# A recurrence stage rewritten: sums on column groups, W x kept in order of time, the state's product added on VectorE

## The chip, the cores and the metric

The kernel runs on one core of a Trainium2 chip. The metric is the device time of one execution in microseconds; the figure for a kernel is the median of its runs. The engines named below are TensorE (PE in the profile, its weight loads PEld), VectorE (DVE), ScalarE (ACT), GpSimd (POOL) and SyncE (SP), whose queue issues most DMAs. Tiles live in SBUF with 128 partitions, results of products in PSUM[...].

## The reference, cut to what matters

The input is 4 images of 128 channels and 64 x 64 places, all in float32. Layer 0, a convolution with a selective scan, and the attention of layer 1 come first and are not touched. The change is in the last line:

```python
t = t + _L1_attn_ref(_ln_t(t), ...)        # t: 4 images, 4096 tokens, 128 channels
t = t + _L1_ffn_ref(_ln_t(t), W, V, gamma, beta)

def _ln_t(v, eps=1e-5):                    # norm over the 128 channels of a token
    m = mean(v, -1); s = var(v, -1)
    return (v - m) / sqrt(s + eps)

def _L1_ffn_ref(x, W, V, gamma, beta):
    flat = (x @ W.T).reshape(4 * 4096, 128)
    mean, var = flat.mean(0), flat.var(0)  # per channel, over all tokens of all images
    Wx = (flat - mean) * rsqrt(var + 1e-5) * gamma + beta
    y = 0
    for t in range(4096):                  # lax.scan
        y = sigmoid(Wx[:, t] + y @ V.T)
        ys[t] = y
    return ys
```

So there are a norm over channels, a product with W (128 x 128), statistics of that product over all 16,384 tokens, and only then a recurrence in time whose every step needs the one before.

## The kernel before, in words

Channels lie on the 128 partitions and tokens along the free axis. Layer 0 and the attention (`_rational`) each run in an order written out by hand (`manual_schedule`: every engine issues in the order of the source). The attention walks through 4 images of 8 blocks of 512 queries; of a block it keeps A, 32 tiles of 128 keys x 512 queries. At a block's end ScalarE takes A in parts, `PARTS`, with a tanh and an exp for each part (L1384, L1385), and PE sums the weighted values (L1360, one product of 512 columns for each of the 32 tiles). After the last block its closing follows (L1252 to L1268: a copy, two products, a reciprocal, a GpSimd add and the store of the block to `x2` in HBM on SP's queue).

The last stage is `_chunked`. It is not under an order by hand: a planner puts the instructions of each engine in order by its costs. Its parts, in order of time:

- **Load.** X (128 x 4 x 4096) comes from `x2` by four DMAs of 2 MB on SP's queue (L170). The weights come on ScalarE's queue (L115).
- **Norms**, for 16 pieces of 1024 columns: the mean over channels is a product with a 128 x 128 matrix of 1/128 (`avg`; two products of 512 columns, L55), which leaves the mean on all partitions. DVE subtracts it out of PSUM (L1450), ACT squares (L1451), PE averages the squares in the same way (L55), ACT takes the logarithm and the exponential that make 1/sqrt (L70, L71), and DVE multiplies into xn (L1455), a copy of the normalised values *in order of time*: column index (step t, chunk c, image b).
- **Sums over W x:** 32 products of 512 columns with W (L1463), each read once out of PSUM by DVE's BN statistics (L1464) and dropped.
- **Scale:** the statistics are put together (L1466) to a scale and a shift per channel; the scale is multiplied into W, which PE transposes (L1474 to L1478, wsT).
- **Steps.** Time is cut into 64 chunks of 64 steps that run side by side: one step works on 64 chunks x 4 images = 256 columns, in two halves of 128 that form two independent streams. A chunk starts from 16 warm-up steps on the end of the chunk ahead of it. In each step PE adds W's product on xn and V's product on the state in one PSUM tile (L1501, L1513), and ACT takes the sigmoid with the shift as bias (L1514), written over xn. W's products do not need the state; they are issued 5 half-steps ahead.
- **Tail.** y is added to X in 16 pieces of 1024 columns, by turns on DVE and POOL (L1524), and each piece is stored by one DMA of 512 KB (L1527). Beside it a flag is worked out that says whether the warm-up had met the chunks' true ends and the attention's bounds held; `_general` runs where it does not.

Rows of other stages that are used for prices below: L671 (products of layer 0 with a 32-column weight, into column groups of one PSUM tile), L678 (ACT's copy out of PSUM to a strided place), L1230 (DVE's multiply of 512 columns with one operand in PSUM), L1243 (DVE's multiply-add of 512 columns), L1336 and L1349 (POOL's adds).

The functions:

Of the kernel before, what the change touches and what calls it, by code (L numbers as in the profile page):

```python
# [38 lines left out]
WARM = 16  # L39
QB = 512  # L40
PARTS = ((0, 4), (4, 12), (12, 20), (20, 32))
CLOSE_AT = (14, 16, 17, 18, 19, 20, 22)
NORM_AT = (15, 17, 19, 20)
QUERIES_AT = (24, 26)
# [100 lines left out]
@with_exitstack  # L145
def _bounded(
    ctx: ExitStack,
    tc: tile.TileContext,
    flag,
    x1,  # L150
    x, in_wT, conv_w, conv_b, sa_w, sa_b, xpT, xpR, dtwT, dtb, A_quads, Ds,
    on_g, on_b, n1_g, n1_b, out_wT, WtT, WxT, Wt, Wx, bh, Wa, ba, W, WT, VT, gamma, beta,
    out,
):
    nc = tc.nc
    const = ctx.enter_context(tc.tile_pool(name="fconst", bufs=1))
    dram = ctx.enter_context(tc.tile_pool(name="gdram", bufs=1, space=DRAM))
    k = _Consts(tc, const)
    x2 = dram.tile([B, P, L], F32, name="x2")

    with tc.manual_schedule():
        _layer0(tc, k, x, x1, in_wT, conv_w, conv_b, sa_w, sa_b, xpT, xpR, dtwT, dtb, A_quads, Ds,
                on_g, on_b, n1_g, n1_b, out_wT)
    top = const.tile([P, TOPS], F32, name="top")
    with tc.manual_schedule():
        _rational(tc, k, x1, x2, top, Wt, Wx, bh, Wa, ba)
    with tc.tile_pool(name="gresid", bufs=1) as resid:
        X = resid.tile([P, B, L], F32, name="X")
        for b in range(B):
            nc.sync.dma_start(X[:, b, :], x2[b])  # L170
        _chunked(tc, None, flag, top, X, k.ident, k.avg, k.ones, k.eps5, k.load, k.filled,
                 W, WT, VT, gamma, beta, out)


@with_exitstack
# [873 lines left out]
def _rational(ctx, tc, k, x1, x2, top, Wt, Wx, bh, Wa, ba):  # L1049
# [253 lines left out]
    for b in range(B):  # L1303
        upcoming = None
        for s in range(nq):
# [74 lines left out]
                else:  # L1380
                    held["first"] = held["first"], lower("B1", F, 1, E)

            for i, (lo, hi) in enumerate(PARTS):
                nc.scalar.activation(A[:, lo:hi, :], A[:, lo:hi, :], AF.Tanh, bias=b_a)  # L1384
                nc.scalar.activation(A[:, lo:hi, :], A[:, lo:hi, :], AF.Exp)  # L1385
                if i == 0:
                    if turned:

                        F = big.tile([P, 2, L], F32, name="F")
                        for c in range(nq):  # L1390
                            all_keys(F, upcoming, c)
                    ahead(0)
                if hi <= NOW or not more:
                    for jt in range(lo, hi):
                        weighted(jt)
                ahead(i + 1) if i + 1 < len(PARTS) else None
            if more:
                nc.vector.tensor_tensor(A[:, 0, :], held["A"][:, 0, :], held["A"][:, 1, :], ALU.add)
                first = held["first"]
# [17 lines left out]


@with_exitstack
def _chunked(ctx, tc, last, flag, top, X, ident, avg, ones, eps5, load, filled, W, WT, VT, gamma, beta, out):  # L1420

    nc = tc.nc
    wp = ctx.enter_context(tc.tile_pool(name="cw", bufs=1))
    big = ctx.enter_context(tc.tile_pool(name="cbig", bufs=1))
    w2 = ctx.enter_context(tc.tile_pool(name="cw2", bufs=2))

    w = load(wp, W, [P, P], "w")
    wT = load(wp, WT, [P, P], "wT")
    vT = load(wp, VT, [P, P], "vT")
    ga = load(wp, gamma, [P, 1], "ga")  # L1430
    be = load(wp, beta, [P, 1], "be")


    xn = big.tile([P, CT, NC * B], F32, name="xn")
    st = big.tile([P, B * L // MM, 6], F32, name="st")
    flat = xn.rearrange("p t c -> p (t c)")
    with tc.tile_pool(name="cps", bufs=2, space=PSUM) as ps2, tc.tile_pool(
        name="cpsm", bufs=1, space=PSUM
    ) as psm:
        with _ln_exp_table(tc, last):  # L1440
            for b in range(B):
                xb4 = xn.rearrange("p t (c b) -> p b c t", b=B)[:, b]
                for c in range(L // CH):
                    cols = slice(c * CH, (c + 1) * CH)
                    mean_ps = psm.tile([P, CH], F32, name="mean_ps")
                    var_ps = psm.tile([P, CH], F32, name="var_ps")
                    t1 = w2.tile([P, CH], F32, name="t1")
                    sq = w2.tile([P, CH], F32, name="sq")
                    _mm(nc, mean_ps, avg, X[:, b, cols], CH)
                    nc.vector.tensor_tensor(t1, X[:, b, cols], mean_ps, ALU.subtract)  # L1450
                    nc.scalar.activation(sq, t1, AF.Square)  # L1451
                    _mm(nc, var_ps, avg, sq, CH)
                    _rsqrt(nc, sq, var_ps, eps5)
                    nch = CH // CT
                    nc.vector.tensor_tensor(  # L1455
                        xb4[:, c * nch : (c + 1) * nch, :],
                        t1.rearrange("p (c t) -> p c t", t=CT),
                        sq.rearrange("p (c t) -> p c t", t=CT),
                        ALU.mult,
                    )  # L1460
            for m in range(B * L // MM):
                ps = ps2.tile([P, MM], F32, name="wx", tag="wx")
                nc.tensor.matmul(ps, wT, flat[:, m * MM : (m + 1) * MM], start=True, stop=True)  # L1463
                nc.vector.bn_stats(st[:, m, :], ps)  # L1464
        mv = wp.tile([P, 2], F32, name="mv")
        nc.vector.bn_aggr(mv, st.rearrange("p a s -> p (a s)"))  # L1466
        scale = wp.tile([P, 1], F32, name="scale")
        _rsqrt(nc, scale, mv[:, 1:2], eps5)
        nc.vector.tensor_tensor(scale, scale, ga, ALU.mult)
        shift = wp.tile([P, 1], F32, name="shift")  # L1470
        nc.vector.tensor_tensor(shift, mv[:, 0:1], scale, ALU.mult)
        nc.vector.tensor_tensor(shift, be, shift, ALU.subtract)

        nc.vector.tensor_scalar(w, w, scale, None, ALU.mult)  # L1474
        ws_ps = ps2.tile([P, MM], F32, name="ws_ps", tag="wx")
        nc.tensor.transpose(ws_ps[:, 0:P], w, ident)
        wsT = wp.tile([P, P], F32, name="wsT")
        nc.vector.tensor_copy(wsT, ws_ps[:, 0:P])  # L1478


    pst = ctx.enter_context(tc.tile_pool(name="cpst", bufs=7, space=PSUM))
    psf = ctx.enter_context(tc.tile_pool(name="cpsf", bufs=1, space=PSUM))
    half = NC * B // 2
    start = wp.tile([P, NC * B], F32, name="start")
    nc.vector.memset(start, 0.0)


    steps = []
    for i in range(WARM):
        t = CT - WARM + i  # L1490
        for lo, hi in ((B, half), (half, NC * B)):
            y = start[:, lo:hi] if i == WARM - 1 else w2.tile([P, half], F32, name="y", tag=f"y{lo}")[:, 0 : hi - lo]
            steps.append((xn[:, t, lo - B : hi - B], y, hi - lo, i == 0))
    for t in range(CT):
        for lo, hi in ((0, half), (half, NC * B)):
            steps.append((xn[:, t, lo:hi], xn[:, t, lo:hi], half, False))

    def project(i):
        rhs, _, n, alone = steps[i]
        ps = pst.tile([P, half], F32, name="wxs")  # L1500
        nc.tensor.matmul(ps[:, 0:n], wsT, rhs, start=True, stop=alone)  # L1501
        return ps

    AHEAD = 5
    queue = [project(i) for i in range(AHEAD)]
    prev = [None, None]
    for i, (_, y, n, alone) in enumerate(steps):
        if i + AHEAD < len(steps):
            queue.append(project(i + AHEAD))
        ps = queue.pop(0)  # L1510
        if not alone:
            state = start[:, (i % 2) * half : (i % 2 + 1) * half] if i in (2 * WARM, 2 * WARM + 1) else prev[i % 2]
            nc.tensor.matmul(ps[:, 0:n], vT, state, start=False, stop=True)  # L1513
        nc.scalar.activation(y, ps[:, 0:n], AF.Sigmoid, bias=shift)  # L1514
        prev[i % 2] = y


    for b in range(B):
        for c in range(L // CH):
            cols = slice(c * CH, (c + 1) * CH)  # L1520
            nch = CH // CT
            eng = nc.vector if c % 2 else nc.gpsimd
            xo = X[:, b, cols].rearrange("p (c t) -> p c t", t=CT)
            eng.tensor_tensor(  # L1524
                xo, xo, xn.rearrange("p t (c b) -> p b c t", b=B)[:, b, c * nch : (c + 1) * nch, :], ALU.add
            )
            nc.sync.dma_start(out[b, :, cols], X[:, b, cols])  # L1527
    gap = wp.tile([P, NC * B - B], F32, name="gap")
    nc.vector.tensor_tensor(gap, xn[:, CT - 1, 0 : NC * B - B], start[:, B:], ALU.subtract)
    worst = wp.tile([P, 1], F32, name="worst")  # L1530
    nc.vector.tensor_reduce(worst, gap, AX.X, ALU.max, apply_absolute_value=True)
    nc.vector.tensor_scalar(worst, worst, MEET, None, ALU.is_le)
# [3 lines left out]
    nc.vector.tensor_scalar(far, far, REACH, None, ALU.is_le)  # L1536
    nc.vector.tensor_tensor(worst, worst, far, ALU.mult)
    n_ps = psf.tile([1, 1], F32, name="n_ps")
    nc.tensor.matmul(n_ps, worst, ones[:, 0:1], start=True, stop=True)
    nc.vector.tensor_copy(flag, n_ps)  # L1540


# [66 lines left out]
```

## Time and profile before

| | us |
|---|---|
| median of 3 runs (lowest, highest) | 11821.63 (11802.34, 11826.4) |
| profiled execution, its own time | 11810.23 |
| its span | 11808.5 |
| of it, up to the end of the last softmax's sum | 11493.6 |
| closing and first of X | 15.4 |
| norms | 120.1 |
| sums over W x | 34.2 |
| scale | 5.3 |
| warm-up steps | 21.8 |
| 64 steps | 74.1 |
| tail | 44.0 |

The span is the time between the first and the last event that the profiler recorded; times within it are counted from its start. The page of the profile gives the busy time of every engine and cuts the span into 40 slices with a digit for each engine. The groups of instructions by line give a count, the busy time and the mean duration of one. A table of windows gives busy time, count, the granted TensorE clock (PEclk, 1.00 is full) and the DMA traffic of chosen stretches. A timeline lists the instructions in order of time: start, duration, engine, line, operation, written tile <- read tiles, shape, and in brackets the idle time before it and what ended that. "PE 10343.2 (88%)" on the page is the busy share of the whole span. The stage that is changed is the last 315 us of it.

### The profile page before, as it was taken

What the parts mean: (1) busy time and instruction counts of PE and PEld (TensorE: products, weight loads), DVE (VectorE), ACT (ScalarE), POOL (GpSimd) and SP (SyncE); (2) the same over time, 40 slices, a digit from 0 to 9 for tenths busy, and PEclk for the clock granted to TensorE, in tenths of its full rate; (3) what the DMA queues carried; (4) which work ended last, traced back from release to release, by engine and by line L of the source; (5) the groups of instructions that cost most, each with busy time, mean ns of one, the idle gap of its engine ahead of it and who ended that gap; (6) DMA issues with size and microseconds to landing.
All of it is one profiled execution on the core that took longest, in us unless ns stands there. A gap on an engine that the chain in (4) does not pass through costs nothing.

```text
span 11808.5 us, 111596 instructions
## 1 busy us (share of the span) xinstructions
PE 10343.2 (88%) x36083; PEld 3200.5 (27%) x36083; DVE 9180.8 (78%) x10131; ACT 9429.7 (80%) x10096; POOL 8599.9 (73%) x3648
## 2 busy tenths in 40 slices
PE   5687787677776699999999999999999999999986
PEld 2121122122111133333333333333333333333324
DVE  4999899889989677777777777777777777777763
ACT  3455555555555599999999999999999999999985
POOL 2898889889889677767767776767677667767751
PEclk8898898889888899999999999999999999999998
DMA  4778778778778300000000000000000000000001
GB/s 107 180 180 193 172 175 187 171 174 188 178 168 189 87 1 3 6 3 3 6 3 3 3 6 3 3 3 6 3 3 6 3 2 3 4 2 2 4 17 43
DMA packets 224900, 737.83 MB, mean 62 GB/s; under 512 B 41056, under 2 KB 42016, under 8 KB 223792
## 3 DMA queue, kind: packets, MB, share of 16 engines
q1 hardware_dynamic: 221184, 729.96, 26.2%
q8 instruction: 285, 4.67, 0.2%
q14 instruction: 311, 2.55, 0.1%
q10 hardware_dynamic: 3120, 0.64, 0.0%
HBM read 613.01 MB, written 117.44 MB: 62 GB/s over the span
## 4 chain that ended last, share of the span: by engine, by line
PE 49%; ACT 10%; DVE 4%; issue 3%; POOL 0%; DMA 0%; DVEq 0%; POOLq 0%; SPq 0%; ACTq 0%
PE pn L1215 26%; PE pd L1215 15%; ACT A L1384 3%; PE ct L1360 3%; ACT A L1385 2%; DVE rb L1230 2%; ACT rb L1234 1%; ACT rb L1235 1%; PE ct L1137 1%; ACT ra L1234 1%; PE wxs L1501 0%; DVE A L1346 0%; DVE rb L1242 0%; PE pn L55 0%; PE ct L1265 0%
## 5 line engine op out<-in xcount | busy, mean ns | idle before, releaser
L1215 PE MATMUL pn<-cE,F 32*128 32x512 f32 (+1 forms) x12288 | 4724.9, 649 | 193.1 <-DVE rb L1230 85.4
L1230 DVE TENSOR_TENSOR rb<-rb,pn 128x512 f32<-128x512 f32 x3972 | 2543.1, 682 | 1310.3 <-PE pd L1215 684.2
L1215 PE MATMUL pd<-E,F 32*128 32x512 f32 (+1 forms) x12288 | 3474.6, 648 | 24.7 <-DVE ra L1242 19.5
L1349 POOL TENSOR_TENSOR ra<-ra,rb 128x1024 f32<-128x1024 f32 x993 | 2634.3, 2653 | 953.1 <-DVE rb L1230 952.7
L1336 POOL TENSOR_TENSOR ra<-ra,rb 128x1024 f32<-128x1024 f32 x993 | 2347.5, 2364 | 407.1 <-DVE rb L1230 347.2
L629 POOL TENSOR_TENSOR dBu<-dtdu,bbcc 128x1024 f32<-128x1024 f32 x1024 | 2398.2, 2368 | 273.8 <-DMA dtdu<-ddd 154.1
L1235 ACT ACTIVATE rb<-rb 128x1024 f32<-128x1024 f32 x1986 | 2100.3, 1058 | 62.8
L1215 PEld LDWEIGHTS pn<-cE,F 32*128 32x128 f32 (+1 forms) x12288 | 1416.3, 185 | 2571.4 <-DVE rb L1230 1067.5
L1234 ACT ACTIVATE rb<-pd 128x1024 f32<-128x1024 f32 x1986 | 2007.7, 1011 | 83.2 <-PE pn L1215 69.9
L671 PE MATMUL py<-h,gather 128*32 128x512 f32 x4096 | 1304.2, 702 | 479.7 <-POOL h L654 381.8
L1230 DVE TENSOR_TENSOR ra<-ra,pn 128x512 f32<-128x512 f32 x1986 | 1315.6, 683 | 230.3 <-ACT ra L1235 183.9
L1215 PEld LDWEIGHTS pd<-E,F 32*128 32x128 f32 (+1 forms) x12288 | 930.6, 185 | 1642.4 <-issue 884.3
L624 ACT ACTIVATE pa<-dtdu,a_neg 128x1024 f32<-128x1024 f32 x1024 | 1144.9, 1118 | 52.4 <-DVE h L644 31.3
L654 POOL TENSOR_TENSOR h<-h,bbcc 128x1024 f32<-128x1024 f32 x384 | 924.1, 2406 | 351.2 <-ACT carry L652 343.7
L644 DVE TENSOR_TENSOR_SCAN pa<-pa,carry,dBu 128x1024 f32<-128x1024 f32 x480 | 1125.2, 2344 | 21.8 <-ACT pa L624 11.3
L1235 ACT ACTIVATE ra<-ra 128x1024 f32<-128x1024 f32 x993 | 1049.5, 1057 | 31.4
L1360 PE MATMUL ct<-A,xT 128*128 128x512 f32 x2048 | 1046.8, 639 | 11.1 <-ACT A L1385 11.0
L1234 ACT ACTIVATE ra<-pd 128x1024 f32<-128x1024 f32 x993 | 1008.8, 1016 | 59.4 <-PE pd L1215 27.4
L652 ACT COPY carry<-pa 128x1 f32<-128x1 f32 x640 | 102.4, 160 | 1120.8 <-DVE h L651 1119.4
L1346 DVE TENSOR_TENSOR A<-ra 128x512 f32<-128x512 f32 x993 | 743.4, 749 | 116.1 <-POOL ra L1336 115.7
L651 DVE TENSOR_TENSOR h<-pa,bbcc 128x1024 f32<-128x1024 f32 x640 | 783.8, 1225 | 60.4 <-DVE pa L644 1.8
L644 DVE TENSOR_TENSOR_SCAN h<-pa,carry,dBu 128x1024 f32<-128x1024 f32 x288 | 674.9, 2343 | 124.1 <-PE py L671 80.4
(286 smaller groups left out, 8832.5 us busy)
## 6 DMA issues: line engine op xcount, KB each, us to landing
bbcc<-bcd SPq DMA_DIRECT2D x1024, 256.0 KB, 7.0
dtdu<-ddd SPq DMA_DIRECT2D x1024, 256.0 KB, 7.1
ddd<-dd SPq DMA_DIRECT2D x64, 1024.0 KB, 5.1
src<-src SPq DMA_DIRECT2D x64, 512.0 KB, 8.1
xs<-in_x_dram SPq DMA_DIRECT2D x16, 512.0 KB, 7.5
src<-xs SPq DMA_DIRECT2D x16, 512.0 KB, 3.0
bcd<-bc SPq DMA_DIRECT2D x64, 128.0 KB, 2.1
src<-xsT SPq DMA_DIRECT2D x16, 512.0 KB, 4.4
```

The lines of the kernel that those rows point to most:

```text
L624: nc.scalar.activation(dA, its[m].DT[r][:, 0, :], AF.Exp, scale=a)
L629: nc.gpsimd.tensor_tensor(dBu, its[m].DT[r][:, 1, :], its[m].BC[q][:, 0, :], ALU.mult)
L644: nc.vector.tensor_tensor_scan(to[:, step], dA[:, step], live.pop(("dBu", u))[:, step], 0.0 if m % nch == 0 else its[m - 1].carry[:, col : ...
L654: nc.gpsimd.tensor_tensor(h, h, cc, ALU.mult)
L671: nc.tensor.matmul(it.y[to, c], gather, live["h", v][:, c], start=False, stop=(q == QS - 1))
L1215: nc.tensor.matmul(ps[a], F[lo:hi, i, jt * P : (jt + 1) * P], side[lo:hi, i, :], start=True, stop=True)
L1230: nc.vector.tensor_tensor(r[:, a, :], r[:, a, :], ns[a], ALU.mult)
L1234: nc.scalar.activation(r, d, AF.Ln, scale=LOWER)
L1235: nc.scalar.activation(r, r, AF.Exp, scale=-1.0)
L1336: nc.gpsimd.tensor_tensor(rA_, rA_, rB2_, ALU.add)
L1349: nc.gpsimd.tensor_tensor(rA, rA, rB1, ALU.add)
L1360: nc.tensor.matmul(ct, xT[:, jt, :], A[:, jt, :], start=(jt == 0), stop=(jt == JT - 1))
```

## The change

- The last stage is put under an order by hand, and X is loaded in 8 spans of 1 MB inside it.
- **Norms and W x in one pipeline** over 8 spans of 2048 columns. A span's mean is made by four products with a 32-column piece of `avg`, each on its own 512 columns and into its own group of 32 partitions of one PSUM tile (`sums`); ACT copies that tile to SBUF (`rows`). A product of one row with ones (K = 32, `sel`, of which only the first row of each group is 1) spreads a group's row to all 128 partitions (`spread`). The variance goes the same way: ACT takes Ln and Exp of one 128 x 512 tile for 2048 columns. Then comes the product with W.
- **W x is kept.** DVE takes the BN statistics from PSUM as before, and ACT copies W x out of PSUM into Z, in order of time. The normalised x is not stored in order of time any more, and there is no scaled W: the scale is applied in the steps.
- **A step** is a product of V with the state in PSUM (pool of 4 instead of 7), a multiply-add on VectorE, u = Z x scale + V y, and ACT's sigmoid of u with the shift as bias, written over Z.
- **Residual sums** are made on GpSimd in each step (all but the last), 256 elements a partition with stride; the last step's by four adds on DVE. Then the 16 output DMAs are issued.
- The last block of the attention takes its softmax in `LAST_PARTS`. W's untransposed load goes.

```diff
+LAST_PARTS = ((0, 8), (8, 16), (16, 24), (24, 29), (29, 32))
...
-    with tc.tile_pool(name="gresid", bufs=1) as resid:
-        X = resid.tile([P, B, L], F32, name="X")
-        for b in range(B):
-            nc.sync.dma_start(X[:, b, :], x2[b])
-        _chunked(tc, None, flag, top, X, ...)
+    with tc.manual_schedule():
+        _chunked(tc, k, flag, top, x2, W, WT, VT, gamma, beta, out)
...
-            for i, (lo, hi) in enumerate(PARTS):
+            for i, (lo, hi) in enumerate(PARTS if more else LAST_PARTS):
...
+    GC = 4 * MM
+    spans = [(b, h) for b in range(B) for h in range(L // GC)]
+    for b, h in spans:
+        nc.sync.dma_start(X[:, b, h * GC : (h + 1) * GC], x2[b, :, h * GC : (h + 1) * GC])
+    nc.scalar.preload_act_table_set("natural_log_exp_and_others")
...
+        class Span:
+            def sums(self, src):
+                ps = pss.tile([P, MM], F32, name="s")
+                for j in range(4):
+                    nc.tensor.matmul(
+                        ps[j * Q : (j + 1) * Q, :], k.avg[:, 0:Q], src[:, j * MM : (j + 1) * MM],
+                        start=True, stop=True,
+                    )
+                return ps
+            def spread(self, rows, pair):
+                ps = psb.tile([P, 2, MM], F32, name="b")
+                for i in range(2):
+                    to = slice((2 * pair + i) * Q, (2 * pair + i + 1) * Q)
+                    nc.tensor.matmul(ps[:, i, :], sel[to, :], rows[to, :], start=True, stop=True)
+                return ps.rearrange("p a q -> p (a q)")
+            def mean(self):
+                self.x = X[:, self.b, self.h * GC : (self.h + 1) * GC]
+                self.rows = w2.tile([P, MM], F32, name="rows")
+                nc.scalar.copy(self.rows, self.sums(self.x))
+            def centre(self):
+                self.t = pt.tile([P, GC], F32, name="t")
+                for pair in range(2):
+                    c = slice(2 * pair * MM, 2 * (pair + 1) * MM)
+                    nc.vector.tensor_tensor(self.t[:, c], self.x[:, c], self.spread(self.rows, pair), ALU.subtract)
+                self.sq = w2.tile([P, GC], F32, name="sq")
+                nc.scalar.activation(self.sq, self.t, AF.Square)
+            def rate(self):
+                ps = self.sums(self.sq)
+                self.rs = w2.tile([P, MM], F32, name="rs")
+                nc.scalar.activation(self.rs, ps, AF.Ln, bias=k.eps5)
+                nc.scalar.activation(self.rs, self.rs, AF.Exp, scale=-0.5)
+            def scale(self):
+                for pair in range(2):
+                    ...
+                    nc.vector.tensor_tensor(self.t[:, c], self.t[:, c], self.spread(self.rs, pair), ALU.mult)
+            def project(self, j):
+                ps = psz.tile([P, MM], F32, name="z")
+                nc.tensor.matmul(ps, w_t, self.t[:, j * MM : (j + 1) * MM], start=True, stop=True)
+                ...
+                nc.vector.bn_stats(st[:, m, :], ps)
+                ...
+                nc.scalar.copy(z4[:, self.b, lo : lo + MM // CT, :], ps.rearrange("p (c t) -> p c t", t=CT))
+        todo = [Span(b, h) for b, h in spans]
+        n = len(todo)
+        for i in range(n + 2):
+            if 0 <= i - 1 < n:
+                todo[i - 1].rate()
+            if i < n:
+                todo[i].mean()
+            if i >= 2:
+                todo[i - 2].project(0)
+                todo[i - 2].project(1)
+            if 0 <= i - 1 < n:
+                todo[i - 1].scale()
+            if i >= 2:
+                todo[i - 2].project(2)
+                todo[i - 2].project(3)
+            if i < n:
+                todo[i].centre()
...
-        nc.vector.tensor_scalar(w, w, scale, None, ALU.mult)
-        ws_ps = ps2.tile([P, MM], F32, name="ws_ps", tag="wx")
-        nc.tensor.transpose(ws_ps[:, 0:P], w, ident)
-        wsT = wp.tile([P, P], F32, name="wsT")
-        nc.vector.tensor_copy(wsT, ws_ps[:, 0:P])
...
+    def step(z, y, state):
+        n = z.shape[-1]
+        if state is None:
+            nc.scalar.activation(y, z, AF.Sigmoid, bias=shift, scale=scale)
+            return
+        ps = pst.tile([P, half], F32, name="vy")
+        nc.tensor.matmul(ps[:, 0:n], v_t, state, start=True, stop=True)
+        u = pt.tile([P, half], F32, name="u")
+        nc.vector.scalar_tensor_tensor(u[:, 0:n], z, scale, ps[:, 0:n], ALU.mult, ALU.add)
+        nc.scalar.activation(y, u[:, 0:n], AF.Sigmoid, bias=shift)
...
     for t in range(CT):
-        for lo, hi in ((0, half), (half, NC * B)):
-            steps.append((xn[:, t, lo:hi], xn[:, t, lo:hi], half, False))
...
+        for a, (lo, hi) in enumerate(((0, half), (half, NC * B))):
+            step(Z[:, t, lo:hi], Z[:, t, lo:hi], prev[a])
+            prev[a] = Z[:, t, lo:hi]
+        if t < CT - 1:
+            nc.gpsimd.tensor_tensor(x4[:, :, :, t], x4[:, :, :, t], z4[:, :, :, t], ALU.add)
     for b in range(B):
+        nc.vector.tensor_tensor(x4[:, b, :, CT - 1], x4[:, b, :, CT - 1], z4[:, b, :, CT - 1], ALU.add)
         for c in range(L // CH):
...
+            nc.sync.dma_start(out[b, :, c * CH : (c + 1) * CH], X[:, b, c * CH : (c + 1) * CH])
```

## The prediction

> **What bounds the kernel now.** I read the 40 slices first: TensorE is nearly full until the last three slices, and the change touches only those. So I cut the end into its stages with a table of windows (row by row: the last softmax, its closing and the load of X, the norms, the sums over W x, a gap, the warm-up steps, the 64 steps, the tail).
>
> ```profile
> core 0: us, PE busy (x) PEld busy (x) DVE busy (x) ACT busy (x) POOL busy (x), PEclk, DMA share, GB/s
> 11452.50:11493.60 41.10, 30.02 (x64) 12.47 (x64) 1.98 (x3) 30.29 (x10) 4.51 (x2) 0.92 0.00 0
> 11493.60:11509.00 15.40, 3.20 (x4) 0.80 (x4) 5.31 (x6) 0.00 (x0) 1.26 (x1) 0.66 0.52 182
> 11509.00:11629.10 120.10, 73.35 (x128) 27.04 (x128) 50.18 (x32) 93.22 (x81) 0.00 (x0) 0.86 0.12 51
> 11629.10:11663.30 34.20, 33.37 (x64) 10.78 (x64) 22.36 (x32) 0.00 (x0) 0.00 (x0) 0.91 0.00 0
> 11663.30:11668.60 5.30, 1.31 (x5) 1.05 (x6) 1.90 (x6) 3.11 (x5) 0.00 (x0) 0.72 0.00 0
> 11668.60:11690.40 21.80, 21.03 (x137) 18.23 (x136) 0.00 (x0) 11.67 (x32) 0.00 (x0) 0.91 0.00 1
> 11690.40:11764.50 74.10, 73.64 (x498) 64.12 (x498) 0.42 (x1) 47.13 (x128) 0.38 (x1) 1.00 0.00 1
> 11764.50:11808.50 44.00, 0.19 (x2) 0.09 (x2) 36.73 (x13) 0.00 (x0) 35.58 (x8) 0.54 0.49 193
> ```
>
> See that ACT leads the norms (93 of 120 us, 32 table loads of 1.283 us in it) and PE the steps (73.6 of 74.1). In the steps PE does W and V for two streams, and the last ones, where no W is left, show the bare chain. The timeline:
>
> ```profile
> 11667.76 3.75 PE L1501 MATMUL wxs<-xn,wsT 128*128 128x124 f32 x16 [0.48 <-DVE wsT L1478]
> 11668.56 0.80 ACT L1514 ACTIVATE y<-wxs,shift 128x124 f32<-128x124 f32 x2 [1.08 <-PE wxs L1501]
> ...
> 11762.20 0.74 PEld L1513 LDWEIGHTS wxs<-xn,vT 128*128 128x128 f32 x4 [0.21 <-ACT xn L1514]
> 11763.15 0.74 PEld L1513 LDWEIGHTS wxs<-xn,vT 128*128 128x128 f32 x4 [0.21 <-ACT xn L1514]
> 11764.08 33.28 DVE L1524 TENSOR_TENSOR X<-X,xn 128x1024 f32<-128x1024 f32 x8 [96.46 <-ACT xn L1514]
> 11764.12 35.96 POOL L1524 TENSOR_TENSOR X<-X,xn 128x1024 f32<-128x1024 f32 x8 [261.06 <-ACT xn L1514]
> ```
>
> Without W a step takes 11763.15-11762.20 = 0.95 us at full clock: ACT 0.37, PE 0.49, the rest hand-over. With W it takes 74.1/64 = 1.16. At half clock the first lone product takes 0.80 (11667.76 to 11668.56), 0.30 more. Which clock the steps get therefore matters; windows of one 3.41 us clock interval each show when it is withdrawn:
>
> ```profile
> 11563.27:11566.69 3.42, 1.98 (x4) 1.00 0.00 0
> 11566.69:11570.10 3.41, 0.78 (x2) 1.00 0.00 0
> 11570.10:11573.51 3.41, 3.41 (x5) 0.50 0.00 0
> 11590.58:11593.99 3.41, 1.98 (x4) 1.00 0.00 0
> 11593.99:11597.41 3.42, 0.03 (x1) 1.00 0.00 0
> 11597.41:11600.82 3.41, 3.41 (x4) 0.50 0.00 0
> ```
>
> A 512-column instruction streams 0.43 us (64 in the sums pass at that pace). Four in an interval (1.71 us, 50%) keep the full clock; two or one lose it in the next. Counted over all 3443 intervals of the trace, full clock was kept above and lost below 37 to 38% of the interval streamed, with about 1% of exceptions; at half clock twice that share is needed to get it back.
>
> **What the Trainium skill says.** "TensorE: Matmul & The Clock Gate", Part 1: half clock after an idle window of some 3.4 us, full after a busy one. The trace agrees, and adds the 37%. The same page, Part 3: matmuls on separate 32-column groups run side by side, three of them 2.38 times faster. The page's nearest row, L671 (four groups), has 4096 instructions in 1304 us busy, where 0.43 each would be 1751: they overlap. "ScalarE: Activation LUTs", What ACT_TABLE_LOAD costs: 1283 ns and a drain of some 1380; here the load is 1283 and the next ACTIVATE starts 0.03 later, so I use 1.28. "VectorE: DVE Perf Modes", Mode 2×_2P: an operand in PSUM excludes the doubled mode; here every PSUM operand costs 0.68 for 512.
>
> **The change part by part**, against the profiled execution (span 11808.5, own time 11810.2).
>
> *Last softmax.* Parts of 8, 8, 8, 5, 3 tiles. A tanh and exp pair costs 7.25 for 8 tiles (11457.69 to 11464.94), 10.75 for 12, so 0.25 and 0.875 a tile: 29.3 in place of 29.1. PE weighs at 0.86 a tile, and ends 10.6 behind the last exp now. With the new parts it is behind by its own backlog, some 7. Gain 3.4. Each queue keeps its order.
>
> *Load of X.* In the built order the store of x2 now stands ahead of X's loads on SP, so the first load issues 2.4 us later after the last product than now (it waits for POOL's 1.26 add and the store's issue). It is 1 MB instead of 2 MB: 2.5 us less at the 0.41 MB/us that the load shows. Gain 0.6, bounds -1.5 to 2.5. Weights' loads (four, not five) are long landed. Sum of both: **-4.0**.
>
> *Norms and W x, one pipeline of 8 spans of 2048 columns.* In the built order a table load still stands ahead of every Ln and every Exp, 16 in the spans in place of 32. Each span depends on the one before through PE's and DVE's order: from the end of one Square to the next. Ln's table 1.28 beside the sums (four column groups, 0.11 + 0.86 + 0.17 = 1.13), Ln 0.68, table 1.28, Exp 0.63: 3.95 with hand-overs. Meanwhile PE does the next span's sums and two products. Then spread 1.2, two multiplies from PSUM at 1.22, two BN statistics at 0.70 queued ahead of the next centring, two subtractions at 1.22, Square of 2048 at 1.95: 13.5. ACT's four copies of W x into Z (0.58 contiguous, 1.05 for the strided row L678; even 1.9 fits nearly) are hidden by the 8 us of DVE. At half clock PE's front (1.92 + 1.71 + 3.42) takes the place of the 3.95, and the spread doubles: 17.5. PE idles some 6 us per span, so the clock falls in each: I take 15. In all 9.3 to the first Square, 7 x 15, and 16 for the last span's rate, scaling and products: 130 (all full clock 116, all half 148) against 154.3 now (11509.0 to 11663.3). **-24.**
>
> *Scale to first sigmoid:* the folding of the scale into W (transpose, copy) goes; two queued copies into Z ahead of Ln's table come. **0** of 5.3, within 1 either way.
>
> *Steps.* PE loses W. VectorE's multiply-add comes onto the chain: 128 columns by L1243's 0.69 for 512 is 0.155 + 0.133 = 0.29 (the PSUM copy of 128 columns at L1478 took 0.29), and a hand-over of 0.04; ACT reads SBUF, 0.03 more. Full clock: 0.95 + 0.36 = 1.30. But two streams then stream 4 x 0.107 = 0.43 us per 1.30, which is **33%, below the 37%**. The clock goes to half, PE takes 0.79 in place of 0.49, a step 1.60, and 27% (full-clock worth) keeps it there. 79 products in a row: 126 and 0.4 for the first sigmoid, against 95.9 now (11668.6 to 11764.5). **+31** (at full clock +7).
>
> *Residual.* 63 adds on POOL of 256 elements: 1.27 for 512 and 2.36 for 1024 give 0.7; the strided L1524 row, which waited for DVE half of the time, gives at most 1.13. Both are inside a step of 1.60, beside ACT and PE. DVE reads one operand from PSUM: L1230, in the same position beside POOL, stays at 0.68. At the end four small adds on DVE (0.3 to the first output), then all 8.4 MB leave at once: 16 DMAs at 0.41 MB/us, 20.5 and 1 for the first bytes. Now the last byte lands at 11803.7 and the span ends 4.8 later; with that, 26.5 in place of 44.0. **-17.5** (3 either way). The flag's chain (4 us) is inside it.
>
> Sum: -4.0 - 24 + 0 + 31 - 17.5 = **-14.5**: span 11794. The runs' median 11821.6 stands 11.4 above the profiled execution; the same above 11794 + 1.7 is 11807.
>
> **The rivals.** *The clock stays full in the steps* (it counts something that a short product has more of): -38 in all, 11783. For it: no stage here runs lone 128-column products for long. Against: intervals that had mostly weight loads and little streaming (15% at 876 us) did not regain it. *The norms stay warm*: 116, -28, 11793. Against: those 6 us. *Column groups run one after another*, on the other side: each set of sums 3.42 instead of 0.86, two per span on the chain, 16 x 2.57 = +41, 11848. It decides once the sums cost over 38 us more, so only if no two groups overlap; L671 speaks against it. *POOL becomes the bound* if a strided add costs over 1.6: at 2.0 it adds 63 x 0.4 = 25, to 11832. That the edit does not do what it says shows in the table loads already, and they are counted.
>
> **How the numbers follow.** As worked out 0.62 (0.13 of it beyond 0.2% faster, as the span stage alone has 14 either way); full clock in the steps 0.14; warm norms 0.12, half of it beyond; serial groups 0.06; slow POOL 0.06, most of it no change. A difference of 0.2%, 24 us, is about what a measurement of this kernel can tell from none. Faster 0.33, same 0.60, slower 0.07. The range 11778 to 11836 takes in the first rival, 14 us of the norms and most of the POOL case, and leaves out serial groups and both clocks full.
>
> **What would show it.** Right: steps 1.60 apart at clock 0.50 with DVE's 0.29 in each; spans 15 apart with 16 table loads; 26 us of tail at 400 GB/s. Wrong: PEclk 1.00 in the steps, sums of 3.4, or POOL behind ACT.

## The result and the profile after

The changed kernel takes 11809.7 us (median of 12 runs, 11800.6 to 11822.8), the kernel before 11822.0 in the runs beside it: a ratio, estimated from all the runs and not from the two medians, of 0.9994 with a 95% interval of 0.9985 to 1.0003. No change can be told from that; 11807 and "the same" were forecast. The profiled execution has a span of 11801.3 us against 11808.5.

Behind the small difference stand four large ones. This is the table of windows of the changed kernel, cut as in the prediction: the last softmax, closing and load, norms with W x, scale, warm-up steps, 64 steps, tail.

```profile
core 0: us, PE busy (x) PEld busy (x) DVE busy (x) ACT busy (x) POOL busy (x), PEclk, DMA share, GB/s
11451.00:11489.10 38.10, 29.29 (x64) 12.72 (x64) 2.02 (x4) 30.65 (x12) 4.48 (x2) 0.87 0.00 0
11489.10:11505.70 16.60, 3.20 (x4) 0.80 (x4) 5.49 (x8) 0.00 (x0) 1.26 (x1) 0.64 0.36 120
11505.70:11637.40 131.70, 90.88 (x320) 24.91 (x320) 58.04 (x64) 80.26 (x79) 0.00 (x0) 0.75 0.12 52
11637.40:11642.90 5.50, 0.00 (x0) 0.00 (x0) 1.77 (x5) 5.41 (x8) 0.00 (x0) 0.77 0.00 0
11642.90:11669.30 26.40, 20.80 (x64) 15.71 (x64) 10.60 (x31) 12.82 (x32) 0.00 (x0) 0.50 0.00 0
11669.30:11775.50 106.20, 88.62 (x254) 62.97 (x253) 44.08 (x128) 51.44 (x128) 73.09 (x63) 0.50 0.00 0
11775.50:11801.30 25.80, 0.19 (x2) 0.09 (x2) 2.39 (x11) 0.00 (x0) 0.00 (x0) 0.50 0.84 328
```

See PEclk: 0.75 in the norms (0.86 and, in the sums over W x, 0.91 before), 0.50 in all 80 steps (0.91 in the warm-up steps and 1.00 in the 64 before). The part ahead of these stages, which the change does not touch, ends anywhere from 11440.7 to 11468.8 us in the profiled executions of this study. Stages of the same code repeat much better: the scale and the steps to 0.1 us or so, the last softmax to 0.5, the load and the tail to about 1, the norms, which meet the clock's intervals differently each time, to 2. So the kernels are compared below by stages, counted from the last softmax's table load:

| us | softmax | load | norms | scale | steps | tail | sum |
|---|---|---|---|---|---|---|---|
| before | 41.0 | 15.5 | 154.2 | 5.3 | 95.9 | 44.0 | 355.9 |
| changed | 38.0 | 16.7 | 131.7 | 5.5 | 132.6 | 25.8 | 350.3 |
| forecast for it | 37.6 | 14.9 | 130.2 | 5.3 | 126.9 | 26.5 | 341.4 |

The step, in the timeline of the changed kernel (start, duration, engine, line; in this and the later timelines TensorE's weight loads are left out, and of the norms also lines of other engines):

```profile
11726.12 0.40 ACT L1547 ACTIVATE Z<-u,shift 128x128 f32<-128x128 f32 x1 [0.64 <-DVE u L1546]
11726.37 0.35 DVE L1546 SCALAR_TENSOR_TENSOR u<-Z,scale,vy 128x128 f32<-128x128 f32 x1 [0.28 <-PE vy L1544]
11726.58 1.42 PE L1544 MATMUL vy<-Z,vT 128*128 128x128 f32 x4 [0.25 <-ACT Z L1547]
11726.75 0.40 ACT L1547 ACTIVATE Z<-u,shift 128x128 f32<-128x128 f32 x1 [0.22 <-DVE u L1546]
11727.22 1.16 POOL L1563 TENSOR_TENSOR X<-X,Z 128x256 f32<-128x256 f32 x1 [0.51 <-ACT Z L1547]
11727.41 0.35 DVE L1546 SCALAR_TENSOR_TENSOR u<-Z,scale,vy 128x128 f32<-128x128 f32 x1 [0.70 <-PE vy L1544]
11727.80 0.40 ACT L1547 ACTIVATE Z<-u,shift 128x128 f32<-128x128 f32 x1 [0.65 <-DVE u L1546]
```

One stream's sigmoid comes at 11726.12 and again at 11727.80, over all 64 steps 1.67 apart. No engine is full in it; the time is a chain from product to VectorE to sigmoid and back. From the start of the product (11726.58) to VectorE's start (11727.41) it takes 0.83 us; that this is due to the half clock is what the experiments have to show.

A span of the norms, from one Square to the next:

```profile
11542.95 1.91 ACT L1484 ACTIVATE sq<-t 128x2048 f32<-128x2048 f32 x1 [0.94 <-DVE t L1482]
11544.87 1.28 ACT L1489 ACT_TABLE_LOAD   x1
11544.91 1.93 PE L1460 MATMUL s<-sq,avg 128*32 128x512 f32 x8 [4.27 <-ACT sq L1484]
11546.61 1.84 PE L1460 MATMUL s<-X,avg 128*32 128x512 f32 x8
11546.91 0.69 ACT L1489 ACTIVATE rs<-s,eps 128x512 f32<-128x512 f32 x1 [0.75 <-PE s L1460]
11547.61 1.28 ACT L1490 ACT_TABLE_LOAD   x1
11548.38 1.98 PE L1499 MATMUL z<-t,wT 128*128 128x512 f32 x4
11548.91 0.63 ACT L1490 ACTIVATE rs<-rs 128x512 f32<-128x512 f32 x1
11550.30 1.14 PE L1470 MATMUL b<-rs,sel 32*128 32x512 f32 x8
...
11557.38 1.91 ACT L1484 ACTIVATE sq<-t 128x2048 f32<-128x2048 f32 x1 [0.94 <-DVE t L1482]
```

The clock of PE over its first two sets of sums, and over what follows them:

```profile
11544.91:11548.20 3.29, 3.29 (x16) 0.50 0.00 0
11548.20:11551.40 3.20, 3.20 (x17) 1.00 0.00 0
```

A set of sums, eight instructions of 512 columns, takes 1.93 us just after 4.27 us of idle, at half clock, where one after the other they would take 8 x 0.85 = 6.8: the column groups overlap. In this span, the shortest, half clock lasts through the sums, and W's products behind them run at full clock again; in the longest spans it lasts through most of the products too. The exponential ends at 11549.54 and PE's two products of W at 11550.3; the spread starts behind PE, not behind ACT. From Square to Square the spans are 14.7, 15.1, 14.4, 15.7, 15.0, 15.7 and 14.7 us.

### The profile page after: what moved, and what is told of

Same layout as the page of the kernel before. It is cut to its first block, busy times and chain, and to the rows that moved or that the text cites. A ratio compares the mean times of both kernels' runs of the same rounds, so it can differ in the third digit from the quotient of the medians.

```text
span 11801.3 us, 111380 instructions
## 1 busy us (share of the span) xinstructions
PE 10343.5 (88%) x35890; PEld 3183.3 (27%) x35890; DVE 9190.8 (78%) x10288; ACT 9423.8 (80%) x10098; POOL 8634.0 (73%) x3703
## 4 chain that ended last, share of the span: by engine, by line
PE 49%; ACT 10%; DVE 4%; issue 3%; POOL 0%; DMA 0%; DVEq 0%; POOLq 0%; SPq 0%; ACTq 0%
PE pn L1212 26%; PE pd L1212 15%; PE ct L1357 4%; ACT A L1381 3%; ACT A L1382 2%; DVE rb L1227 2%; ACT rb L1231 1%; ACT rb L1232 1%; PE ct L1134 1%; ACT ra L1231 1%; PE vy L1544 1%; DVE A L1343 0%; DVE rb L1239 0%; PE pn L56 0%; PE ct L1262 0%
```

## The experiments

Theory: the change loses its gain because its steps stream too little to hold the TensorE clock. Rivals: VectorE's new instruction and GpSimd's adds are what makes the step long; and the clock follows something else than the share of the time in which PE streams columns.

**Residual sums moved back behind the steps.**

```diff
-        if t < CT - 1:
-            nc.gpsimd.tensor_tensor(x4[:, :, :, t], x4[:, :, :, t], z4[:, :, :, t], ALU.add)
...
+            eng = nc.vector if c % 2 else nc.gpsimd
+            xo = X[:, b, cols].rearrange("p (c t) -> p c t", t=CT)
+            eng.tensor_tensor(xo, xo, z4[:, b, c * nch : (c + 1) * nch, :], ALU.add)
```

> The changed kernel with the residual sums after the steps, as in the kernel before (16 pieces of 1024 columns, by turns on VectorE and GpSimd, each stored when it is done). Theory (the adds within the steps are covered and cost the steps nothing): steps stay 1.67 apart, the tail is 44 us instead of 26, span some 11820. Rival (GpSimd slows VectorE's instruction in the steps, 0.35 us where 0.29 was forecast): VectorE 0.29 to 0.30, step 1.61, 132.6 falls to 128, span some 11815.

Measured: ratio 1.0010 (1.0001 to 1.0018); steps 132.7, tail 42.8. VectorE's multiply-add in the steps, first in the changed kernel, then in this run:

```profile
L1546 DVE SCALAR_TENSOR_TENSOR u<-Z,scale,vy 128x128 f32<-128x128 f32 x128 | 44.3, 346 | 62.4 <-PE vy L1544 62.4
L1546 DVE SCALAR_TENSOR_TENSOR u<-Z,scale,vy 128x128 f32<-128x128 f32 x143 | 49.5, 346 | 65.4 <-PE vy L1544 64.9
```

346 ns with GpSimd's adds beside it, 346 without them: the adds cost the steps nothing and are worth the 17.0 us of the tail. VectorE's price is its own.

**The clock, by added products.** In the changed kernel PE idles 6.8 us in the pause at the scale and meets the first step at half clock; the question is whether the steps would hold the full one. Behind each product of V one more is issued into a PSUM tile that nobody reads, and some in the pause, so that the steps begin at full clock.

```diff
+    for _ in range(7):
+        nc.tensor.matmul(idle, v_t, X[:, 0, 0:MM], start=True, stop=True)
...
         nc.tensor.matmul(ps[:, 0:n], v_t, state, start=True, stop=True)
+        nc.tensor.matmul(idle[:, 0:128], v_t, X[:, 0, 0:128], start=True, stop=True)
```

> The changed kernel with one more product of 128 columns, into a tile that nobody reads, behind each product of V, and seven of 512 columns in the pause ahead of the steps; all else is as in the changed kernel. Theory (the clock is withdrawn because too little is streamed): PE now streams 8 x 0.107 = 0.86 us a step, some 63% of it, so the clock stays at 1.00 in the steps, V's product takes 0.49 instead of 0.79, the step 1.37 instead of 1.67, the 79 steps 24 us less: span some 11777, ratio to the kernel before about 0.997. Rival (the clock follows something else, or the chain is DVE and ACT alone): clock 0.50 as before, step 1.67 or longer since the added product stands ahead of the other stream's, span 11801 or more.

Measured: ratio 1.0082 (1.0069 to 1.0096), steps 231.9. The run missed both expectations through a fault of its own: the added products read X, into which GpSimd writes in every step, and PE waited 1.25 us for that in nearly every one of the 64 steps. A step grew to 3.3 us, and the clock fell (0.50 from 11670 to 11860). Its warm-up steps, where GpSimd has nothing to do, are a clean test: the clock stays at 1.00 and the sigmoids of one stream come 1.35 apart. PE over the warm-up steps:

```profile
11643.00:11664.00 21.00, 19.32 (x127) 1.00 0.00 1
```

> As the run with the added products of 128 columns, but of 16 columns: PE streams 0.43 + 4 x 0.013 = 0.48 us in a step of 1.37, 35%. Theory (full clock needs more than 37 to 38% of an interval streamed): the steps begin at 1.00 and fall to 0.50 within the first intervals, 1.67 a step for nearly all of them, span some 11800. Rival (the count of products is what keeps the clock): 1.00 through the steps, 1.37 a step, as with 128 columns.

Measured in one execution: span 11846.4. The windows of PE, the first over the first warm-up steps:

```profile
core 0: us, PE busy (x), PEclk, DMA share, GB/s
11658.90:11663.50 4.60, 3.24 (x24) 0.97 0.00 0
11663.50:11700.00 36.50, 31.30 (x138) 0.50 0.00 0
```

With 35% streamed (an estimate, worked out in the expectation) the clock is gone at 11663.5 and stays away, with nothing but 16 columns for 128 changed. In the warm-up steps, ahead of GpSimd's first add, the sigmoids of one stream are 1.35 apart, then 1.71. The number of products is not what keeps the clock.

The same with a constant tile in place of X:

```diff
-        nc.tensor.matmul(idle[:, 0:128], v_t, X[:, 0, 0:128], start=True, stop=True)
+        nc.tensor.matmul(idle[:, 0:128], v_t, k.ones, start=True, stop=True)
```

> As the first run with added products of 128 columns, but they read a constant tile of ones and not X, which GpSimd writes in every step; and 28 products of 128 columns stand in the pause. Theory (in the first such run the added products waited for GpSimd's write to X, which alone made its steps 3.3 us; the clock follows the streamed share): clock 1.00 through the steps, 1.35 a step as in the warm-up steps of that run, steps 107 us instead of 132.6, all other stages as in the changed kernel, ratio to the kernel before about 0.997. Rival (the added products hold up the other stream's product on PE): 1.35 + 0.2 a step and more, steps 123 us.

Measured: ratio 0.9971 (0.9960 to 0.9983); steps 108.6, the other stages as in the changed kernel. Of its timeline:

```profile
11701.03 0.40 ACT L1551 ACTIVATE Z<-u,shift 128x128 f32<-128x128 f32 x1 [0.33 <-DVE u L1550]
...
11701.49 0.49 PE L1547 MATMUL vy<-Z,vT 128*128 128x128 f32 x2
...
11702.02 0.35 DVE L1550 SCALAR_TENSOR_TENSOR u<-Z,scale,vy 128x128 f32<-128x128 f32 x1 [0.39 <-PE vy L1547]
```

The product of V is back to 0.49 us, and from its start to VectorE's it takes 0.53 instead of 0.83. PE does twice the products and the steps take 24 us less: these 24 of the 36.7 us that the change added to the steps are the lost clock, and more streaming keeps it. The other 12.7 (108.6 against 95.9 before) stay at full clock; what they are shows when VectorE's instruction goes out of the steps again, below.

> As the run with added products of 128 columns on a constant tile, but of 32 columns: PE streams 4 x 0.107 + 4 x 0.027 = 0.53 us in a step of 1.36, 39%. Theory (full clock is kept above 37 to 38% of an interval): clock 1.00 through nearly all steps, 1.36 a step, steps some 109 us. Rival (the bound lies higher for short products, or many short ones don't count as streaming): the clock falls as with 16 columns, 1.67 to 1.71 a step, steps 132 to 136.

Measured in one execution: span 11772.0, steps 108.6; PE's window in them:

```profile
11640.00:11740.00 100.00, 91.23 (x588) 1.00 0.00 1
```

So the full clock is kept with an estimated 39% of the time streamed and lost with 35%. The two runs were executed once each; the steps with 128 and with 32 added columns agree at 1.36 us.

**W's product back on PE.** The steps are those of the kernel before; norms, GpSimd's adds and tail those of the change.

```diff
-                nc.scalar.copy(z4[:, self.b, lo : lo + MM // CT, :], ps.rearrange("p (c t) -> p c t", t=CT))
+                nc.scalar.copy(z4[:, self.b, lo : lo + MM // CT, :],
+                    self.t[:, j * MM : (j + 1) * MM].rearrange("p (c t) -> p c t", t=CT))
...
-    pst = ctx.enter_context(tc.tile_pool(name="cpst", bufs=4, space=PSUM))
+    pst = ctx.enter_context(tc.tile_pool(name="cpst", bufs=6, space=PSUM))
...
+        nc.tensor.matmul(ps[:, 0:n], wsT, rhs, start=True, stop=alone)
...
+    AHEAD = 5
...
+            nc.tensor.matmul(ps[:, 0:n], v_t, state, start=False, stop=True)
+        nc.scalar.activation(y, ps[:, 0:n], AF.Sigmoid, bias=shift)
```

> The changed kernel with the steps of the kernel before: ACT copies the normalised x to its place in order of time where it copied W x, W is scaled and transposed again, PE adds W's product and V's in PSUM, and there is no VectorE instruction in the step; norms, GpSimd's residual adds within the steps and the tail stay those of the changed kernel. Theory (the multiply-add on VectorE and the lost clock are the whole loss of the change): steps 1.16 apart at clock 1.00, 95.5 us instead of 132.6, norms and tail as in the changed kernel (132 and 26), span some 11764, ratio to the kernel before about 0.996. Rival (GpSimd's adds, 1.16 us each in the changed kernel, become the bound or disturb the steps): over 1.20 a step, and GpSimd ends some us behind the last sigmoid.

Measured: ratio 1.0095 (1.0080 to 1.0111), steps 262.1; neither expectation. The timeline, and the clock over the first steps:

```profile
11657.95 0.36 ACT L1573 ACTIVATE y<-wxs,shift 128x124 f32<-128x124 f32 x1 [1.37 <-PE wxs L1572]
11658.36 0.79 PE L1560 MATMUL wxs<-Z,wsT 128*128 128x124 f32 x2 [0.51 <-ACT y L1573]
11658.94 0.64 PE L1572 MATMUL wxs<-y,vT 128*128 128x128 f32 x2
11659.68 0.37 ACT L1573 ACTIVATE y<-wxs,shift 128x128 f32<-128x128 f32 x1 [1.37 <-PE wxs L1572]
```

```profile
11652.40:11655.10 2.70, 1.42 (x8) 1.00 0.00 0
11655.10:11658.30 3.20, 2.20 (x8) 0.55 0.00 0
11658.30:11700.00 41.70, 29.33 (x97) 0.50 0.00 0
```

W's product, which should run ahead of the state, waits for the sigmoid just before it ("<-ACT y"). Five products ahead and one in use fill the six tiles, so the next one needs the tile that this sigmoid reads. The two streams became one chain of 1.2 us a half-step at full clock; that streams an estimated 0.86 us in 2.4, 36%, and the clock fell too. The remedy is one tile more; W's transpose takes a tile of this pool first:

```diff
-    pst = ctx.enter_context(tc.tile_pool(name="cpst", bufs=6, space=PSUM))
+    pst = ctx.enter_context(tc.tile_pool(name="cpst", bufs=7, space=PSUM))
...
-    ws_ps = psf.tile([P, P], F32, name="ws_ps")
+    ws_ps = pst.tile([P, half], F32, name="wxs")
```

> As the run with W's product on PE, but with 7 PSUM tiles in the steps' pool, as the kernel before has, instead of 6; W's transpose takes one of them. Theory (with 6 tiles and 5 products ahead, each product of W waited for the sigmoid of the half-step just ahead, which made the two streams one chain of 1.73 us a half-step, and the clock fell with it): steps 1.16 apart at clock 1.00, 96 us, as in the kernel before, with GpSimd's adds (1.16 each) just inside; with the norms at 128, as in that run, the time from the last softmax on is 355.9 - 3.0 - 26.0 - 18.0 + 2 = 311 us, ratio to the kernel before about 0.996. Rival (GpSimd's adds are the bound or slow the sigmoids): steps over 1.20, GpSimd ends over 2 us behind the last sigmoid.

Measured: ratio 0.9952 (0.9939 to 0.9966); steps 95.4, tail 27.2, sum 312.3 where 311 was expected. One PSUM tile more is worth 167 us. At full clock and without VectorE's instruction the steps are back to the time before, so the 12.7 us that the added products left go with its place on the chain (they themselves add nothing visible: 32 columns gave the same 108.6 as 128). GpSimd keeps up, but only just:

```profile
L1577 POOL TENSOR_TENSOR X<-X,Z 128x256 f32<-128x256 f32 x63 | 73.0, 1163 | 165.2 <-ACT Z L1573 164.8
```

The idle time in this line is nearly all the wait for the first add; between the adds GpSimd is idle for 0.2 us in all. 63 adds of 1.163 us are 73.3 us in 64 steps of 1.16, and the last ends 0.6 behind the last sigmoid. A little longer, and it would be the bound.

**The parts of the last softmax alone**, put into the kernel before:

> The kernel before with nothing but the parts of the last softmax changed to those of the changed kernel (8, 8, 8, 5, 3 tiles). Theory: the parts alone make the gain of that stage; from the last softmax's table load to the end of the weighted sum 38.0 us instead of 41.0, and all later stages stay as in the kernel before. Rival (part of the gain is the order by hand of the new stage behind it): 39 us or more, or a later stage moves.

Measured in one execution: 38.0 us, where the kernel before has 41.0. The parts are the whole gain of that stage. Of the stages whose code is the same as before, the load took 16.5 (15.5 before), the norms 156.2 (154.2) and the tail 43.1 (44.0), the scale and the steps the same: so much a stage moves by itself.

**One table load instead of sixteen.**

```diff
-    nc.scalar.preload_act_table_set("natural_log_exp_and_others")
...
             def rate(self):
+                if self.b == self.h == 0:
+                    nc.scalar.preload_act_table_set("natural_log_exp_and_others")
                 ps = self.sums(self.sq)
```

> The changed kernel with its preload of the table that has both logarithm and exponential moved from the start of the stage to just ahead of the first logarithm; in the built order no table load is left in the norms but that one, and none ahead of the scale (16 + 2 before). Theory (in a span PE's own queue, two sets of sums and two products of W, ends as late as ACT's exponential, so that ACT's loads are covered in the inner spans; only the first and last span and the scale show them): 2.6 us at the scale, 1.3 in each of the first and last span, norms 129 instead of 131.7, span of each inner one 14.9 as now; in all 4 to 6 us less. Rival (ACT's loads are on the chain of every span): 1.3 us for each of 8 spans and 2.6, 13 us less, norms 121.

Measured: ratio 0.9987 (0.9981 to 0.9994); norms 128.3, scale 2.9, sum 344.2, 6.1 less. The 2.6 at the scale are clear. The norms are 3.3 less than in the changed kernel, but only 1.3 less than the shortest with all sixteen loads (129.6 to 131.7). Inner spans stay at 14.5 to 15.8 us, as in the changed kernel; only the first is shorter (12.6, where runs with the loads had 13.8 to 14.7). ACT's loads are covered in the inner spans, as PE's queue ends later.

**The last store of x2 on ScalarE's queue.**

```diff
-            nc.sync.dma_start(x2[b, :, blocks[s]], xr)
+            (nc.sync if parts > 1 else nc.scalar).dma_start(x2[b, :, blocks[s]], xr)
```

> The changed kernel with the last store to x2 issued from ScalarE's queue, so that the loads of X on SP's queue do not stand behind it and its wait for GpSimd's add. Theory (that place in the queue delays the first load by 2.4 us): the first load is issued at the end of the closing's second product, 7.5 us behind the weighted sum instead of 9.9, and the load stage is 14.3 us instead of 16.7. Rival (what holds the first MB is the start of the transfers, not their issue): issue is earlier and the first MB lands at the same time, 16 to 17 us.

Measured in one execution: load 15.2 instead of 16.7, and neither expectation. The first load was issued 9.5 us behind the weighted sum (9.9 in the changed kernel), not 7.5. SyncE's waits in this run say what held it:

```profile
SPq L1431 <- POOL xr L1264: 16.6, 1, 16.6
```

The load itself waits for GpSimd's add, with no store ahead of it. Only 0.4 of the 2.4 us were the queue. (Why it has to wait is open: X may lie over a tile that the add uses; not tried.) But PE could start on it 5.7 us after its issue instead of 6.8. The two combined runs below repeat both figures within 0.1, with loads of 15.3 us.

**Together, and with the clock held in the norms too.**

> The run with W on PE and 7 PSUM tiles, with the table's preload just ahead of the first logarithm and the last store on ScalarE's queue. Theory (the effects lie in different stages and add up): from the last softmax on 312.3 - 6.1 - 2.4 = 304 us (355.9 in the kernel before), ratio to the kernel before about 0.9945. Rival (without its table loads ACT's copies to Z come earlier and the span is bound by PE, so the table brings only the 2.6 at the scale): 307 us.

Measured: ratio 0.9957 (0.9943 to 0.9970); sum 307.0. Against the run with 7 tiles the scale is 1.3 less, the norms 1.4, the load 2.1 and the tail 1.1. That is the rival's number, but not its reason: it expected all of the table's gain, 2.6, at the scale.

Then the products added to the norms, in `sums` and `rate`:

```diff
+                for _ in range(extra):
+                    nc.tensor.matmul(ps, k.avg, self.x[:, 0:MM], start=True, stop=True)
...
-                ps = self.sums(self.sq)
+                ps = self.sums(self.sq, 4 if self.b or self.h else 2)
```

> The combined run with four more products of 512 columns (two in the first span) in PE's idle time while ACT squares, into the tile that the sums overwrite. Theory (PE idles over 4 us a span, loses its clock there, and its sums, products and spreads at half clock are what a span waits for): clock near 1.00 in the norms, a span some 13.2 instead of 14.5 to 15, norms 10 to 13 us less than in the combined run (some 115), ratio to the kernel before about 0.9935. Rival (VectorE, ACT and hand-overs bound the span at any clock): norms within 3 us of the combined run, or longer where the added products overrun the pause.

Measured: ratio 0.9949 (0.9935 to 0.9963); norms 111.0, sum 289.6. The window of the norms, and a span (its first line are the four added products, in two instructions each, while VectorE and ACT are at work):

```profile
11514.60:11625.60 111.00, 100.38 (x380) 32.96 (x380) 58.13 (x64) 60.11 (x65) 0.00 (x0) 0.96 0.16 64
```

```profile
11545.00 3.70 PE L1460 MATMUL s<-X,avg 128*128 128x512 f32 x8
11547.38 1.91 ACT L1486 ACTIVATE sq<-t 128x2048 f32<-128x2048 f32 x1 [4.26 <-DVE t L1484]
11549.34 1.06 PE L1462 MATMUL s<-sq,avg 128*32 128x512 f32 x8 [0.64 <-ACT sq L1486]
...
11560.20 1.91 ACT L1486 ACTIVATE sq<-t 128x2048 f32<-128x2048 f32 x1 [4.23 <-DVE t L1484]
```

Clock 0.96, the same eight instructions of the sums 1.06 us for 1.93, most spans 12.8. Products whose results nobody needs save 16.5 us of the 127.5 that the norms took in the combined run. By stages this is the fastest kernel of the study, 66.3 us below the kernel before. The timed intervals of the last three kernels overlap, because the part ahead of the stages moves by more than their differences; the stages tell them apart, the medians don't.

## Why the prediction was right, point by point

- **Last softmax**, -3.4 forecast: -3.0 measured, and the parts alone make it.
- **Load of X**, -0.6: **+1.2**, or +0.3 against the 16.5 of the kernel before with other parts. The term was wrong in two places. The delay of the issue was foreseen in its size (9.9 us behind the weighted sum for 7.5), but its reason was only in small part the store ahead in the queue: the load waits for GpSimd's add by itself, as the run with the store elsewhere showed. And the 1 MB was priced at the steady rate, 5.5 us from issue to landing; it took 6.8:

```profile
11498.54 0.32 SPq L1265 DMA_DIRECT2D x<-xr  x1
11498.96 5.16 SPq L1431 DMA_DIRECT2D X<-x  x8
11505.75 1.93 PE L1460 MATMUL s<-X,avg 128*32 128x512 f32 x8 [9.30 <-DMA X<-x]
```

  (The figures are from the issue to PE's first product.) With the store on the other queue it took 5.7 to 5.8 in three executions, near the price. So the store just ahead of it in the same queue goes with the missing 1.1 us; how it costs them was not taken apart.
- **Norms**, -24 (130): -22.5 (131.7), good to about 2. To the end of the first Square 9.3 were forecast and 9.3 measured, for the end 16 and 17.0. The seven spans of 15 (15.05 measured) were not worked out but chosen between 13.5 at full clock and 17.5 at half. The trace shows why the middle was about right. PE idles 4.3 us ahead of the sums, not 6, and its front, from the sums to the spread, was forecast at 7.05 for half clock throughout; in the six spans behind the first it took 5.4 to 6.7 us, as only 3.3 to 5.9 of them were at half clock. In the run that kept the clock it took 3.8, which shows what the falling clock costs. Which part of the new pipeline makes the rest of the gain (column groups, half the table loads, the order by hand) no run takes apart.
- **Scale**, 0: +0.2. 2.6 of its 5.5 us are the table loads that the run with one load is without.
- **Steps**, +31: **+36.7**. Right in its mechanism, half clock because 33% is too little, and wrong in one price. VectorE's multiply-add was put at 0.29 us from a slope of 512 columns and a fixed part of another operation; it takes 0.346. From 346 ns at 128 columns and 687 at 512 (L1243, a like instruction), an estimate is 0.89 ns a column and 0.23 us fixed, where the prediction had 0.155 fixed. The price makes 0.056 of the 0.07 us by which the step is longer than 1.60, 79 times. The forecast for full clock, 1.30 a step, came out as 1.35 for the same reason.
- **Residual and tail**, -17.5: -18.2, good to about 1. An add on GpSimd takes 1.16 us, just above its upper bound of 1.13, and is hidden at 1.67, at 1.35, and still at 1.16 a step.

The stages add up to -5.6 instead of -14.5; the profiled execution started them 1.5 us earlier, which makes the -7.2 of the span. The forecast median is 2.7 us from the measured one, and that is luck: the stages missed by 8.9. The part ahead of them, which the change does not touch, gave back 1.5, and the median stands 6.7 above the profiled execution's own time (11803.0), where 11.4 had been taken over from the kernel before, which gave back 4.7. The forecast of no change did not hang on it: 14.5 and 5.6 us less are both inside the 24 us that the prediction took for the least that a measurement can tell.

Of the rivals, serial column groups fall with the 1.93 us of a set of sums, GpSimd as the bound with the run that moved its adds behind the steps. Full clock in the steps and full clock in the norms did not happen, and both were then brought about: in the steps it was worth 24.0 us, where the two prices differed by 24 (+31 and +7), in the norms of the combined kernel 16.5 us, where 14 was put.

## What to carry to other kernels

Work that is taken off TensorE can cost more than it saves when what is left no longer holds the clock: add up the streamed time per clock interval before and after, as a share of it, and look for the share at which the clock falls. In this case it lay between 36% (lost) and 39% (kept), and below it the product on the chain took 0.83 us instead of 0.53. Keeping W's product on PE, or filling PE with products that nobody reads, beat removing it. And count the PSUM tiles of a look-ahead: five half-steps ahead, with two streams by turns and W's product issued ahead of V's, took seven tiles (262.1 us of steps with six, 95.4 with seven). By the order of issue that is n + 2 for n half-steps ahead; other n were not tried. With one too few the look-ahead turns into a wait for the consumer just before.

## What the runs showed of the hardware that was not expected

- Very small products are enough to hold the full clock: 32 columns added per half-step (39% streamed, an estimate like the two that follow) kept 1.00 over 100 us, with 16 columns (35%) it was lost within 5 us. A chain at 36% lost it as well. In "TensorE: Matmul & The Clock Gate", Part 1, the Trainium skill has half clock after an idle window; in the run with 16 columns it came with PE never idle for a whole interval.
- Eight instructions of 512 columns on four column groups take 1.06 us at full clock, a factor of 3.2 below 8 x 0.43, and 1.93 us at half clock.
- The table with logarithm and exponential is loaded once in the norms where its preload stands just ahead of the first logarithm, and sixteen times where it stands at the start of the stage, ahead of the first copies and squares: a matter of the order in the program. It was worth 2.6 us at the scale and 1.3 to 3.3 in the norms.
